# Two-layer recurrent block: final norms and silu at once behind the experts, and 2.3 attention pieces a pair instead of 2

## The chip, the core and the metric

The kernel runs on one core of one Trainium2 chip. TensorE (PE in the profile) multiplies matrices, with its weight loads shown as PEld; VectorE (DVE), ScalarE (ACT) and GpSimd (POOL) work on tiles in the on-chip memory; SyncE (SP) issues most of the transfers. Each engine runs its own instructions in order, and semaphores tie the engines together. The metric is the device time of one execution in microseconds (us).

## What is computed

16 sequences of 256 tokens with 128 values each go through two layers. Each layer normalizes its input, computes a mixer `s` and a mixture of experts `g` from the same normalized input, and adds `s * silu(g)`. The change touches layer 1 alone:

```python
xn = _layernorm(x)
s = _L1_attn_ref(xn, w_qkv, w_proj)          # causal attention, 16 heads of 8, 256 tokens
g = _silu(_L1_ffn_ref(xn, ...))              # 16 experts, two per token
x = x + s * g

def _L1_ffn_ref(x, ...):
    scores = einsum('btd,nd->btn', x, router_w) + router_bias
    topv, topi = top_k(scores, 2)
    weights = softmax(topv)
    ...
    hidden = tanh(mag) * cos(softplus(freq) + 0.1 + bank_phase)
    ...
    out = einsum('tkd,tk->td', sel, weights)
    out = out * rsqrt(mean(out * out, -1) + 1e-6) * norm_w
    return out
```

So the expert half needs a sum over a token's two experts, a norm of that sum and a silu; only then does it meet the attention's `s`, in a product, and `x` in a sum.

## The kernel before

All 4096 tokens are held as 8 blocks of 512 (`NB`), each block as 4 tiles of 128 tokens (`NTL`). `xs[b]` is a block of `x`, `xns[b]` its normalized form (128 of the 130 values of a row of `xnx[b]`), `xnTs[b]` that form transposed. `s_sbs[b]` is another view of the memory of `xnTs[b]`: once a block's attention is done, its `s` takes the place of the transposed input.

Layer 1 has two streams of work that are independent until the end.

*The attention* is a generator of small pieces, `attention()` (L867). It walks over 32 tiles of queries, each in several steps: scores `Sq` to find the maximum (L923, L933, L935), queries with the maximum built in (L985, L987, L991), scores `Sk` again, transposed (L956), their exponential on ACT (L963) with a triangle cut out by POOL for the diagonal (L966), the weighted values `yx` (L1006, copied at L1011), a transpose and the division by the sums (L1018, L1026, L1028). A step's scores for one tile go out with the transposed scores of the tile two before. Per block there are five projections ahead, and a transpose (`turned`, L1038) and the output projection (`projected`, L1046, which copies `s` at L1047 and adds the block to `done`) behind. A piece is yielded with a kind: 0 for a piece that counts, 1 for an exponential, 2 for a mark without work.

*The experts* (L1103) take 79 slots of 128 rows, each of one expert, in ten batches of 8 (the last has 7). A batch gathers its rows, transposes them (L1110), does the frequency products in pairs of tiles (L1121) with abs, exp and ln on ACT (L1125 to L1127) and five DVE operations (L1129 to L1137), loads ACT's other table (L1141), does the magnitude products with a tanh (L1147, L1152), the sines (L1158), loads the first table again (L1159), multiplies (L1164), does the down products (L1173), weighs them (L1177), and scatters the rows to `yd` in DRAM by indirect DMAs on POOL (L389).

`fill(n)` (L1215) puts `n` counting pieces of attention between the steps of the experts. `fill(n, False)`, used in the tanh stage where the table of the exponential isn't loaded, stops at once where the next piece is an exponential. Per batch it is called once at the transposes, with 1 and with `FILL - 1` for every pair in the frequency stage, with `1, False` for every pair in the tanh stage, once behind the sines, and once for each four tiles of the down products. `FILL` is 3. Work that a piece leaves for DVE, such as a maximum, is put into `later` and goes out ahead of the next piece. The order on PE, DVE, ACT and SP is the order in which the Python code issues the instructions; POOL's is held by explicit dependencies.

Behind the experts, `give` sends out the remaining scatters. Then the blocks are finished (`finished`, L1182), in four stages with a `yield` after each: load both results of every token (`results`, L439; the load waits for all scatters of the layer); sum them and take the squares (L1187, L1191) and the factor of the norm (L1192, L1193); scale (L1196), work out the sigmoid in three ACT operations (L1199 to L1201) and multiply by `s` (L1202); multiply by the sigmoid (L1204), add `x` (L1205) and send the block out (L1206). `staged` (L197) runs these as a pipeline: each step of it admits one more block, if `ready` allows, and advances all that are under way by a stage. `ready` asks that the block's attention is done. One step follows every three pieces of attention; what is left when the pieces run out is run behind them.

Of the kernel before, what the change touches and what calls it, by code (L numbers as in the profile page):

```python
# [10 lines left out]
F32 = mybir.dt.float32  # L11
# [3 lines left out]
ALU = mybir.AluOpType  # L15
# [3 lines left out]
P = 128  # L19
D = 128  # L20
# [3 lines left out]
NTL = BT // P  # L24
# [11 lines left out]
SLT = (2 * 4096 + E1 * (P - 1)) // P  # L36
DX = D + 2
WROW = 2 * H1 + 2 * D + 2
FILL = 3
RATE = 0.93  # L40
NEG = -3.0e38
INV2PI = 1.0 / (2.0 * math.pi)
# [10 lines left out]
def ib(ap, n):  # L53
    s = list(ap.shape)
    return ap.unsqueeze(len(s)).to_broadcast(s + [n])
# [3 lines left out]
def two_layer_kernel(  # L59
# [7 lines left out]
    nc = tc.nc  # L67
    NT = x.shape[0]
    NB = NT // BT
# [4 lines left out]
    ov = out.rearrange("(b t p) d -> b p t d", p=P, t=NTL)  # L74
    xs = [cst.tile([P, NTL, D], F32, tag=f"x{b}", name=f"x{b}") for b in range(NB)]

    xnx = [cst.tile([P, NTL, DX], F32, tag=f"xnx{b}", name=f"xnx{b}") for b in range(NB)]
    xns = [t[:, :, 0:D] for t in xnx]
    xnTs = [cst.tile([P, BT], F32, tag=f"xnT{b}", name=f"xnT{b}") for b in range(NB)]

    s_sbs = [t.rearrange("p (t d) -> p t d", t=NTL) for t in xnTs]
# [115 lines left out]
    def staged(gens, ready=lambda b: True):  # L197

        gens, live, b = list(gens), [], 0
        while gens or live:  # L200
            if gens and ready(b):
                live.append(gens.pop(0))
                b += 1
            live = [g for g in live if next(g, g) is not g]
            yield
# [22 lines left out]
    def starts(pool, ne):  # L228

        rm = pool.tile([P, ne * NT32], F32, tag="rt_rm", name="rm")  # L230
        nc.gpsimd.memset(rm, 1.0)
        nc.gpsimd.memset(rm[:, 0 : ne * NT32 : NT32], 0.0)
        return rm
# [197 lines left out]
    def spread():  # L431

        turn[:] = [not turn[0]]
        if wanted and (turn[0] or not given):
            fetch(1)
        else:
            give(1)

    def results(pool, lay, b, tag="gg"):  # L439

        gg = pool.tile([P, 2, NTL, D], F32, tag=tag, name="gg")
        for c in range(2):
            r0 = c * 4096 + b * BT
            got = nc.sync.dma_start(gg[:, c], yds[lay][r0 : r0 + BT, :].rearrange("(t p) d -> p t d", p=P))
            for give in gives[lay]:
                tc.add_manual_dep(got.ins, give.name, SYNC, reason="results in rows")
        return gg
# [31 lines left out]
    with ExitStack() as cg:  # L479
# [307 lines left out]
        with tc.manual_schedule(engines={ET.Activation, ET.PE, ET.DVE, ET.SP}):  # L787
# [15 lines left out]
            hp = hp0.enter_context(tc.tile_pool(name="ghp", bufs=2, side="right"))  # L803
# [21 lines left out]
    with ExitStack() as c1:  # L825
# [261 lines left out]
        def weights_of(j0, n):  # L1087

            wts = []
            for j in range(j0, j0 + n):  # L1090
                reg = tile_expert(emap1, j, E1)
                wt = hp.tile([P, WROW], F32, tag="wt", name="wt", bufs=CPB + 1)
                nc.sync.dma_start(wt, bank[bass.ds(reg, 1)].rearrange("e p w -> p (e w)"))
                wts.append(wt)
            return wts

        def rows_of(j0, n):

            xg = hp.tile([P, n, DX], F32, tag="xg", name="xg")
            wanted.extend((xg, 1, j0 + i, i) for i in range(n))  # L1100
            return xg

        def experts(j0, n, wts, xg, fill):  # L1103
# [12 lines left out]
            for i0 in range(0, n, 2):  # L1116
                m = 2 * min(2, n - i0)
                pf = pf_.tile([P, 4, P], F32, tag="pf", name="pf")
                for k in range(m):
                    i, c = i0 + k // 2, k % 2  # L1120
                    nc.tensor.matmul(  # L1121
                        pf[:, k, :], wts[i][:, c * P : (c + 1) * P], xgTs[i // 4][:, i % 4, :], start=True, stop=True
                    )
                z = hp.tile([P, 4, P], F32, tag="z", name="z", bufs=2)
                nc.scalar.activation(z[:, :m, :], pf[:, :m, :], AF.Abs)  # L1125
                nc.scalar.activation(z[:, :m, :], z[:, :m, :], AF.Exp, scale=-1.0)
                nc.scalar.activation(z[:, :m, :], z[:, :m, :], AF.Ln, bias=1.0)  # L1127
                fill(1)
                nc.vector.scalar_tensor_tensor(z[:, :m, :], pf[:, :m, :], 0.0, z[:, :m, :], ALU.max, ALU.add)  # L1129
                v = hp.tile([P, 4, P], F32, tag="v", name="vt", bufs=CPB // 2 + 1)  # L1130
                for i in range(m // 2):
                    ks = slice(2 * i, 2 * i + 2)
                    nc.vector.scalar_tensor_tensor(  # L1133
                        v[:, ks, :], z[:, ks, :], INV2PI, ib(wts[i0 + i][:, WROW - 2 :], P), ALU.mult, ALU.add
                    )
                nc.vector.tensor_scalar(z[:, :m, :], v[:, :m, :], MAGIC, MAGIC, ALU.add, ALU.subtract)  # L1136
                nc.vector.tensor_tensor(v[:, :m, :], v[:, :m, :], z[:, :m, :], ALU.subtract)  # L1137
                vs.append(v)
                fill(FILL - 1)

            nc.scalar.preload_act_table_set(TRIG)  # L1141
            for i0 in range(0, n, 2):
# [36 lines left out]
                )  # L1179
                given.extend((og, 1, j0 + i, i) for i in range(i0, i0 + n4))  # L1180

        def finished(b):  # L1182

            gg = results(hp, 1, b, "xg")
            yield
            acc = hp.tile([P, NTL, D], F32, tag="v", name="acc1", bufs=CPB // 2 + 1)
            nc.vector.tensor_tensor(acc, gg[:, 0], gg[:, 1], ALU.add)  # L1187
            sq = hp.tile([P, NTL, D], F32, tag="th", name="sq1", bufs=CPB // 2 + 1)
            ss = hp.tile([P, NTL], F32, tag="ss", name="ss1")
            for t in range(NTL):  # L1190
                nc.scalar.activation(sq[:, t, :], acc[:, t, :], AF.Square, accum_out=ss[:, t : t + 1])  # L1191
            nc.scalar.activation(ss, ss, AF.Ln, bias=eps6, scale=1.0 / D)  # L1192
            nc.scalar.activation(ss, ss, AF.Exp, scale=-0.5)  # L1193
            yield
            for t in range(NTL):
                nc.vector.scalar_tensor_tensor(  # L1196
                    acc[:, t, :], acc[:, t, :], ss[:, t : t + 1], sb_nw, ALU.mult, ALU.mult
                )
            nc.scalar.activation(sq, acc, AF.Exp, scale=-1.0)  # L1199
            nc.scalar.activation(sq, sq, AF.Ln, bias=1.0)  # L1200
            nc.scalar.activation(sq, sq, AF.Exp, scale=-1.0)  # L1201
            nc.vector.tensor_tensor(acc, acc, s_sbs[b], ALU.mult)  # L1202
            yield
            nc.vector.tensor_tensor(sq, sq, acc, ALU.mult)  # L1204
            nc.vector.tensor_tensor(sq, xs[b], sq, ALU.add)  # L1205
            nc.sync.dma_start(ov[b], sq)  # L1206
            yield

        wk_ = c1.enter_context(tc.tile_pool(name="l1wk", bufs=2, side="right"))
        pS = c1.enter_context(tc.tile_pool(name="l1pS", bufs=2, space=PSUM))  # L1210
        ps = c1.enter_context(tc.tile_pool(name="l1ps", bufs=2, space=PSUM))
        pf_ = c1.enter_context(tc.tile_pool(name="l1pf", bufs=2, space=PSUM))
        pieces, ahead, later, done = attention(), [], [], set()

        def fill(n, exps=True):  # L1215

            k = 0
            while k < n:
                spread()
                kind, f = ahead.pop() if ahead else next(pieces, (3, None))  # L1220
                if kind != 1:
                    while later:
                        later.pop(0)()
                if kind == 3:
                    return False
                if kind == 1 and not exps:
                    ahead.append((kind, f))
                    return True
                if f is not None:
                    f()  # L1230
                k += kind == 0
            return True

        ET = mybir.EngineType
        with tc.manual_schedule(engines={ET.Activation, ET.PE, ET.DVE, ET.SP}):
            nc.scalar.preload_act_table_set(LN_EXP)

            c_ps[:] = [pf_, "pf"]
            for _ in cstream:
                fill(3)  # L1240
            with tc.tile_pool(name="rt1", bufs=1) as rt1:
                for _ in route(rt1, pf_, sc1, E1, SLT, 1, emap1, starts(rt1, E1), "pf", {"tag": "pf"}):
                    fill(1)
            ccmb.close()
            hp = c1.enter_context(tc.tile_pool(name="l1h", bufs=2))
            batches = [(j0, min(CPB, SLT - j0)) for j0 in range(0, SLT, CPB)]
            got = weights_of(*batches[0]), rows_of(*batches[0])
            fetch(len(wanted))
            for k, (j0, n) in enumerate(batches):
                now, got = got, None  # L1250
                if k + 1 < len(batches):
                    got = rows_of(*batches[k + 1])
                experts(j0, n, *now, fill)
                fetch(len(wanted))
                if got:
                    got = weights_of(*batches[k + 1]), got
            give(len(given))
            ends = staged([finished(b) for b in range(NB)], lambda b: b in done)
            while fill(3):
                next(ends, None)  # L1260
            for _ in ends:
                pass


# [51 lines left out]
```

## Time and profile before

| | us |
|---|---|
| median of 3 runs | 1236.36 |
| lowest and highest run | 1234.08, 1241.92 |
| the profiled execution | 1251.36 |
| its span, first to last instruction | 1249.60 |
| mean granted TensorE clock | 0.843 |

Busy time over the whole span is 910.2 us on PE (73%), 646.3 on PE's weight loads (52%), 769.5 on DVE (62%), 588.7 on ACT (47%) and 390.2 on POOL (31%).

The places in the span that matter here, all in us from its start:

| | us |
|---|---|
| first transposes of the experts (L1110) | 681.0 |
| second L1177 of the first batch, of the last | 736.6, 1135.4 |
| last scatter issued (L389) | 1142.9 |
| first sum of a block's results (L1187) | 1149.2 |
| sums of the next five blocks | 1155.4, 1162.3, 1172.2, 1179.1, 1187.3 |
| sums of the last two blocks | 1221.5, 1239.0 |
| last output projection's copy (L1047) | 1236.2 |
| last output transfer issued (L1206) | 1246.2 |

A busy share is an average over stages that have different limits. So the page of the profile is read first for the whole, and then by windows, where each stage shows which engine has no time left. Where none has, the chain of waits and the timelines show who waits for whom.

### The profile page before, as it was taken

To read this page: it belongs to the slowest core of one execution; us is meant where nothing else is said; L and a number is where in the kernel's file an instruction comes from. 1 tells how busy PE (TensorE), PEld (TensorE's weight loads), DVE (VectorE), ACT (ScalarE), POOL (GpSimd) and SP (SyncE) were. 2 spreads that over 40 slices of the span, in tenths; PEclk is the share of its full clock that TensorE was granted. 3 is DMA by queue.
4 is the path that set the end of the run, shared out by engine and by line. 5 is a ranking of instruction groups with operands and counts; after the bars stand their busy time and mean duration, and the time that the engine had idled before them with its cause. 6 is when DMAs were issued, how large, how long until landed. Compare 5 with 4: busy or idle time off the path is not lost. (4 is left out here: it accounts for less than half of the span.)

```text
span 1249.6 us, 17774 instructions
## 1 busy us (share of the span) xinstructions
PE 910.2 (73%) x6394; PEld 646.3 (52%) x6394; DVE 769.5 (62%) x1442; ACT 588.7 (47%) x1059; POOL 390.2 (31%) x422
## 2 busy tenths in 40 slices
PE   6756478878787773767374887878897889888673
PEld 4334256666566652554142565566565656665342
DVE  5675455646455546736886655756765766675853
ACT  3331267665657462431131455544454655544643
POOL 2000235454455320000103333633652553443120
PEclk9967689899889885677777887988988989899776
DMA  4040248842333202100403030431331333122211
GB/s 112 1 69 1 64 107 211 165 111 72 97 99 106 62 15 88 51 1 1 69 1 129 20 119 18 136 116 33 124 125 48 100 129 117 25 94 66 84 35 34
DMA packets 88415, 95.41 MB, mean 76 GB/s; under 512 B 22228, under 2 KB 64040, under 8 KB 88328
## 3 DMA queue, kind: packets, MB, share of 16 engines
q1 hardware_dynamic: 78632, 74.32, 21.9%
q0 software_dynamic: 9696, 19.97, 6.1%
q8 instruction: 50, 0.82, 0.3%
q14 instruction: 37, 0.30, 0.1%
HBM read 78.03 MB, written 22.51 MB: 80 GB/s over the span
## 5 line engine op out<-in xcount | busy, mean ns | idle before, releaser
L389 POOL DMA_INDIRECT yd<-og,row x150 | 153.8, 1025 | 240.9 <-DVE og L758 116.6
L377 POOL DMA_INDIRECT xg<-xnd,tok x150 | 148.9, 993 | 155.0 <-DVE yT L646 79.7
L956 PE MATMUL Sk<-qm,kT 32*128 32x256 f32 x768 | 129.1, 460 | 43.3 <-ACT pr L963 20.5
L966 POOL TENSOR_SCALAR_AFFINE_SELECT pr<-pr 128x1024 f32<-128x1024 f32 x64 | 72.0, 1125 | 275.7 <-ACT pr L963 275.3
L963 ACT ACTIVATE pr<-Sk 128x1024 f32<-128x1024 f32 x96 | 97.8, 1019 | 96.9 <-PE Sk L956 94.6
L923 PE MATMUL Sq<-km,qT 32*128 32x256 f32 x768 | 132.6, 457 | 12.1 <-DVE mx L933 4.3
L956 PEld LDWEIGHTS Sk<-qm,kT 32*128 32x128 f32 x768 | 76.2, 214 | 61.7 <-ACT pr L963 29.3
L923 PEld LDWEIGHTS Sq<-km,qT 32*128 32x128 f32 x768 | 70.2, 207 | 58.2 <-issue 35.3
L935 DVE TENSOR_REDUCE negm<-Sq 128x8 f32<-128x1024 f32 x64 | 78.0, 1219 | 30.3 <-PE Sk L956 21.7
L721 PEld LDWEIGHTS pf<-xgT,wt 128*128 128x128 f32 x568 | 77.2, 208 | 31.4 <-issue 15.0
L721 PE MATMUL pf<-xgT,wt 128*128 128x128 f32 x568 | 82.9, 294 | 12.0 <-ACT sg L730 6.3
L726 ACT ACTIVATE sg<-pf,nb 128x128 f32<-128x128 f32 x142 | 44.1, 361 | 62.1 <-PE pf L721 61.2
L737 DVE SCALAR_TENSOR_TENSOR gt<-pf,nb,sg 128x128 f32<-128x128 f32 x142 | 42.8, 344 | 47.1 <-ACT sg L730 47.0
L546 PE MATMUL pq<-xnT,sb_wq 128*128 128x512 f32 x64 | 45.4, 850 | 30.0 <-DVE sp L519 28.5
L917 PE MATMUL Sq<-mq,identb 128*128 128x512 bf16 x128 | 42.0, 412 | 16.7 <-DVE negm L935 10.6
L1129 DVE SCALAR_TENSOR_TENSOR z<-pf,z 128x512 f32<-128x512 f32 (+1 forms) x40 | 27.1, 678 | 43.5 <-ACT z L1127 43.5
L1125 ACT ACTIVATE z<-pf 128x512 f32<-128x512 f32 (+1 forms) x40 | 23.7, 593 | 60.9 <-PE pf L1121 60.9
L1173 PE MATMUL pe<-wt,th 128*128 128x128 f32 x316 | 46.7, 309 | 7.0 <-DVE th L1164 7.0
L1173 PEld LDWEIGHTS pe<-wt,th 128*128 128x128 f32 x316 | 43.4, 220 | 14.0 <-issue 10.9
L754 PE MATMUL pe<-sb_wo,gt 128*128 128x128 f32 x284 | 40.1, 300 | 13.0 <-ACT xgT L700 13.0
L754 PEld LDWEIGHTS pe<-sb_wo,gt 128*128 128x128 f32 x284 | 37.2, 210 | 21.5 <-ACT xgT L700 18.1
L351 PE MATMUL pT<-ohj,ohp 128*128 128x142 bf16 (+1 forms) x128 | 14.7, 275 | 45.4 <-DVE ohj L349 45.4
(269 smaller groups left out, 2114.1 us busy)
## 6 DMA issues: line engine op xcount, KB each, us to landing
wt<-bank SPq DMA_DIRECT2D x79, 385.0 KB
wt<-in_w_dram SPq DMA_DIRECT2D x71, 256.0 KB
gg<-yd SPq DMA_DIRECT2D x32, 256.0 KB
xnd<-xnx SPq DMA_DIRECT2D x16, 260.0 KB
xg<-xnd,tok POOLq DMA_INDIRECT x150, 3.4
yd<-og,row POOLq DMA_INDIRECT x150, 2.5
x<-in_x_dram SPq DMA_DIRECT2D x8, 256.0 KB
bank<-in_freq_dram SPq DMA_DIRECT2D x1, 2048.0 KB
```

The costliest lines, as they stand in the source:

```text
L377: return nc.gpsimd.indirect_dma_start(out=xg[:, i, :], out_offset=None, in_=xnds[lay], in_offset=bass.IndirectOffsetOnAxis(ap=toks[lay][:, ...
L389: give = nc.gpsimd.indirect_dma_start(out=yds[lay], out_offset=bass.IndirectOffsetOnAxis(ap=rows[lay][:, j : j + 1], axis=0), in_=og[:, i, ...
L546: nc.tensor.matmul(pq[:, c], w_[:, h * DK : (h + 1) * DK], xnT, start=True, stop=True)
L721: nc.tensor.matmul(pf[:, c, :], wts[i][:, c * P : (c + 1) * P], xgT[:, i, :], start=True, stop=True)
L726: nc.scalar.activation(sg[:, c, :], pf[:, 2 + c, :], AF.Exp, scale=-1.0, bias=nbs[i][:, 2 + c : 3 + c])
L754: nc.tensor.matmul(pe[:, i, :], gts[i][:, c, :], sb_wo0[:, c, :], start=(c == 0), stop=(c == 1))
L923: nc.tensor.matmul(S[:, c, js, :], qT[part][r, tq], km[r, js, tk], start=not diag, stop=True, skip_group_check=True,)
L935: passed(nc.vector.tensor_reduce(ng, S, AX.X, ALU.max, negate=True))
L956: nc.tensor.matmul(S[:, c, js, :], kT[part][r, tk], qm[r, js, :], start=True, stop=True, skip_group_check=True,)
L963: nc.scalar.activation(pr, S, AF.Exp, scale=scale)
L966: pooled(nc.gpsimd.affine_select(pr_, pr_, pattern=[[0, 8], [1, P]], compare_op=ALU.is_ge, fill=0.0, base=0, channel_multiplier=-1,))
L1173: nc.tensor.matmul(pe[:, i - i0, :], ths[i // 2][:, 2 * (i % 2) + c, :], wts[i][:, 2 * H1 + c * D : 2 * H1 + (c + 1) * D], start=(c == 0), ...
```

## The change

Three things change, all in layer 1.

`FILL` is 2.3, and where `fill(FILL - 1)` gave 2 pieces, a running share now gives 2.3 on average: 2 or 3 pieces, the rest carried on to the next pair.

`finished` is split. `weighed(b)` has its load, sum, norm and sigmoid, and ends with a product of the two into `xns[b]`, whose old content isn't needed any more; it adds the block to `ready`. The new `finished(b)` multiplies that by `s`, adds `x` and sends the block out.

The loop at the end runs `weighed` for all blocks without asking for their attention, one step after every two pieces instead of three, and calls `finished(b)` in order for each block whose attention and weighing have both been issued.

```diff
-FILL = 3
+FILL = 2.3
...
                 vs.append(v)
-                fill(FILL - 1)
+                share[0] += FILL
+                fill(int(share[0]))
+                share[0] -= int(share[0])
...
-        def finished(b):
+        def weighed(b):
...
             nc.scalar.activation(sq, acc, AF.Exp, scale=-1.0)
             nc.scalar.activation(sq, sq, AF.Ln, bias=1.0)
             nc.scalar.activation(sq, sq, AF.Exp, scale=-1.0)
-            nc.vector.tensor_tensor(acc, acc, s_sbs[b], ALU.mult)
-            yield
-            nc.vector.tensor_tensor(sq, sq, acc, ALU.mult)
-            nc.vector.tensor_tensor(sq, xs[b], sq, ALU.add)
-            nc.sync.dma_start(ov[b], sq)
-            yield
+            yield
+            nc.vector.tensor_tensor(xns[b], sq, acc, ALU.mult)
+            ready.add(b)
+            yield
+
+        def finished(b):
+            o = hp.tile([P, NTL, D], F32, tag="z", name="o1", bufs=2)
+            nc.vector.tensor_tensor(o, xns[b], s_sbs[b], ALU.mult)
+            nc.vector.tensor_tensor(o, xs[b], o, ALU.add)
+            nc.sync.dma_start(ov[b], o)
...
+        share, ready = [0.0], set()
...
             give(len(given))
-            ends = staged([finished(b) for b in range(NB)], lambda b: b in done)
-            while fill(3):
+            ends, last, b = staged([weighed(b) for b in range(NB)]), False, 0
+            while b < NB:
+                last = last or not fill(2)
                 next(ends, None)
-            for _ in ends:
-                pass
+                while b in done and b in ready:
+                    finished(b)
+                    b += 1
```

## The prediction

> **What bounds the kernel now.** I read four views, in this order: the busy time by stage, the chain of waits at its end, DVE's timeline behind the experts, and PE's and ACT's there.
>
> The windows, in us, with PE, weight loads, DVE, ACT and POOL, each with its count, then the granted clock and the DMA's share:
>
> ```profile
> 690.00:1135.00 445.00, 369.10 (x3040) 266.44 (x3040) 293.30 (x504) 233.26 (x332) 188.31 (x184) 0.91 0.27 84
> 1149.20:1206.80 57.60, 38.91 (x280) 23.04 (x280) 45.86 (x83) 32.98 (x90) 7.77 (x7) 0.71 0.28 79
> 1206.80:1237.00 30.20, 23.00 (x174) 14.43 (x174) 8.66 (x25) 11.99 (x23) 4.37 (x4) 0.78 0.05 14
> ...
> 1135.00:1144.00 9.00, 8.71 (x83) 5.46 (x86) 5.55 (x9) 2.90 (x4) 6.87 (x8) 1.00 0.14 46
> ```
>
> The experts of layer 1 (690 to 1135) hold PE busy for 83% of their time. From 1149 to 1207 DVE is the fullest engine (45.86 of 57.60): six blocks are finished there beside the attention. From 1207 to 1237 it is PE again.
>
> The chain of waits, at its end (start, length, engine, tile, line):
>
> ```profile
> 1229.89 1.06 DVE acc L1196 x4
> 1230.97 0.64 ACT sq L1199
> ...
> 1235.41 3.47 DMA gg<-yd
> 1238.97 0.70 DVE acc L1187
> 1239.70 1.29 ACT sq L1191 x8
> 1241.57 1.15 DVE acc L1196 x4
> 1242.74 0.64 ACT sq L1199
> 1243.41 0.64 ACT sq L1200
> 1244.07 0.64 ACT sq L1201
> 1244.73 0.70 DVE sq L1204
> 1245.45 0.69 DVE sq L1205
> ```
>
> The end is one block's load, norm and silu, with nothing beside it. None of that except the last two DVE steps needs the attention's result.
>
> DVE's, PE's and ACT's timelines (start, length, line, operation; in brackets the idle time before it and who ended it):
>
> ```profile
> 1149.18 0.69 DVE L1187 TENSOR_TENSOR acc<-gg 128x512 f32<-128x512 f32 x1 [7.10 <-DMA gg<-yd]
> 1154.77 0.69 DVE L1202 TENSOR_TENSOR acc<-acc,xnT 128x512 f32<-128x512 f32 x1 [0.69 <-ACT sq L1199]
> ...
> 1150.53 1.12 PE L1018 MATMUL pyt<-ident,yt 128*128 128x128 f32 x4 [4.86 <-DVE qm L991]
> ...
> 1223.91 1.01 ACT L963 ACTIVATE pr<-Sk 128x1024 f32<-128x1024 f32 x1
> 1236.19 0.59 ACT L1047 COPY xnT<-p_s 128x512 f32<-128x512 f32 x1 [2.16 <-PE p_s L1046]
> ...
> 1224.97 1.93 PE L1006 MATMUL yx<-pr,va 128*32 128x256 f32 x16 [3.06 <-ACT pr L963]
> 1232.93 0.48 PE L1038 MATMUL pyT<-ident,y 128*128 128x128 f32 x1 [2.39 <-DVE y L1028]
> ```
>
> The first block's results come 13.3 us after the last expert product on DVE (1135.9), and DVE stands 7.10 us for them. L1202 overwrites `acc` while ACT's L1199 still reads it: 0.69 us, eight times. Twice a block's norm stands in the attention's way: ACT's squares before the 1223.91 exponential, DVE's L1196 and L1202 before the last transpose.
>
> **Where the attention stands.** I counted its pieces from the code's order: 254 that count in `fill`, with exponentials between them that don't. The ten batches issue 17, 16, 17, 16, 17, 18, 16, 18, 16 and 18, which leaves 47 for the time behind them, the first being the second query projection of block 7. The trace agrees: that matmul (L882) starts at 1135.15, the first on PE behind the experts' last.
>
> **The change, part by part.**
>
> 1. *More attention beside experts.* The second fill of each pair of tiles gives 2.3 pieces on average, not 2: 12 more over 40 pairs. But the tanh stage's `fill(1, False)` returns empty at an exponential, and with the shifted order it does so more often. The same count with the change gives 17, 18, 17, 18, 19, 18, 17, 17, 18, 17: 7 more, not 12. Those seven are what PE does now in 1135 to 1144: 8.71 us of work at clock 1.00, some 9.5 at the experts' 0.91. Nothing hides it surely, since PE is busy 83%. Least: a third falls into PE's 76 us of gaps, +6. Most: a piece costs as much as a whole expert stage divided by its 169 pieces, 445/169 = 2.6 us, +18. I take +10, near the row. The Trainium skill ("Trainium Kernel Development and Optimization", Performance Expectations) holds matmul busy time a bad measure of how near the roof PE is, and weight-load busy a good one. By that the stage is 60% full (266.44/445) and the seven cost perhaps 5 us; the sum below would be 5 us better. I stay with the matmul row, since the engine's queue is in order. Beside this, every batch is rearranged: four batches with 16 pieces each took 48.5, 43.9, 37.6 and 43.1 us (from second product to second product). With a spread of 4.5 us a batch, ten may sum to 10 us either way.
>
> 2. *The first wait.* The order is now 2 pieces, load of block 0, 2 pieces, L1187; before, 3 and 3. The wait for the results (POOL's seven scatters at 1.27 us, their landing, the load's 3.3 us) is unchanged and ends 13.3 us behind the last product, in both. But less stands before L1187: PE can run 6 pieces until then where it ran 8. Queued behind DVE's wait are the maxima, and so PE's next scores and ACT's squares. Against the seven fewer pieces, the wait thus gives back two: 34 pieces remain at its end instead of 39. No time by itself; its price lies in the next part.
>
> 3. *Eight blocks instead of six, beside 16 pieces instead of 21.* From 1149.18 to the end of the last query score (1206.8) DVE worked 45.86 us. Six blocks' finishing in it is some 27 us (L1187 0.69, L1196 1.13 to 1.96, L1202 0.69, L1204 and L1205 1.4 and more), the pieces that now lie ahead of the wait some 4.4, so 14.5 stay for attention. With the change: eight times L1187, L1196 and the new product (2.5) and six times the two final operations (1.4), with 2 us for slow ones as in the trace: 30. Sum 44.5. DVE's idle time was 11.7: 4.2 from L1202's wait, which goes as the product no longer overwrites what ACT reads, and 7 from waiting for PE. I leave 3.5: 48 us, that is -9.5. What is late next is ACT: per block 2.0 us of exponentials, 1.8 of squares and 1.2 of attention, 5 us, against DVE's 5.6 per round. The loads now alternate with output transfers on SP: each load is issued a round (5.6 us) ahead of its use and lands in 3.5, so nothing; without that cover 3.5 us a block. POOL's selects (1.1 us) stand behind the scatters as before. The product's write into rows of 130 values has no row; 0 to 0.1 us each, taken as 0. Bounds of this part: -13 (no idle time) to -4. The lower end is where a rule speaks against the change. After gaps of 4.86 and 3.06 us the trace shows matmuls at 0.80 for 0.48 and at 1.93 for 1.07; clock 0.71 over the stage. The Trainium skill ("TensorE: Matmul & The Clock Gate", Part 1: The HAM clock gate) says that one idle window of about 3.4 us drops the array to half clock and as long a busy one restores it. Rounds with two pieces leave PE idle about half of the time, so by the rule PE stays slow, each round's scores come 0.7 us later, and this part gives -4, the sum -6. I keep the row: the stage has much of that slow clock already, and PE isn't its bound.
>
> 4. *Attention's last 18 pieces.* Block 6's squares no longer delay the exponential of 1223.91 (its scores ended at 1221.9): -2.0. L1196 and L1202 no longer delay the last divide (possible at 1230.1, was 1232.24): -2.1. Block 6's final two operations fit DVE's idle time around 1218. Sum -4.1; perhaps 1.5 more if PE's shorter gap keeps its clock.
>
> 5. *The end.* From the last copy of `s` (1236.78) to the end of the span (1249.6) are 12.8 us. Left are two DVE operations (1.4), semaphores (0.1) and the output transfer, which took 1246.2 to 1249.6, 3.4: 4.9. So -7.9. The loads, squares and exponentials taken from here lie in part 3, counted there.
>
> Sum: +10 - 9.5 - 4.1 - 7.9 = -11.5, with the clock's 1.5 about -13. The profiled execution took 1251.36 (span 1249.60), 15 above the median of the runs shown, 1236.36: profile 1238, median 1223.
>
> **The rivals.**
>
> *The experts stall (slower).* Only one query score and one key score fit PSUM at a time. A third piece between two pairs more often brings a second score, which waits for a maximum on DVE behind L1129 to L1137, itself behind ACT's chain. The trace has such a wait: PE 3.74 us idle before the scores of 1017.10, then slow matmuls (0.80). Were 8 of the 12 third pieces to meet it at 3.7 us: +30 beside the +10, against -21.5 to -23: +18, 1254. It is slower by 1% from 7 such waits on. For it: L956 waits longest for `pr` and `negm`. Against: 40 pairs with three pieces each show few of these gaps now.
>
> *Only the end is gained.* The eight blocks cost in rounds of two pieces what they cost before, part 3 giving nothing: +10 - 4.1 - 7.9 = -2, 1234. For it: DVE and ACT hand each block back and forth three times, and the first wait comes earlier.
>
> *The move is free.* The pieces fill PE's gaps, and batches fall well: +0 for part 1, -23: 1213.
>
> **How the numbers follow.** My forecast has 0.45, the only-end rival 0.25, the free move 0.15, the stall 0.15. The forecast's own uncertainty, mainly the rearranged batches, is some 10 us. The range, 1206 to 1243, takes in the free move and the only-end rival and leaves most of the stall out; the forecast's own is 1213 to 1234. Within 1% (1224 to 1248.7) is about what a measurement can't tell from no change. Faster by more: half of the forecast and its better side, the free move, little of the rest, 0.50. Within: 0.36. Slower: 0.14.
>
> **What would show it.** Right: 7 pieces fewer behind the experts; those about 10 us longer; no L1187 or L1196 behind the last copy of `s`, which is 5 us before the end; DVE over 90% busy from its first wait to the last query score. Wrong: experts longer by over 25 us with L956 waiting for `negm` or `mx`; DVE idle in the rounds for `ss` or `sq`; a load landing late for L1187.

## The result and the profile after

| | us |
|---|---|
| before, median of 20 runs (the 3 shown above among them) | 1241.00 |
| changed kernel, median of 20 runs | 1249.47 |
| ratio, with its 95% interval | 1.0066, 1.0044 to 1.0088 |
| profiled execution of the changed kernel, its span | 1251.8 |

The kernel became slower by two thirds of a per cent, where 1% faster was forecast. (The forecast of 1223 us started from the median of three runs, 1236.36; that of twenty is 1241.00.) The shorter end is there, to about a microsecond. The experts took it back, and more.

Splitting each profiled execution at the second L1177 of the first batch and at that of the last batch gives the two halves of the account. (Between L1137 and L1201 a line of before has a number higher by two in the changed kernel: L1177 is L1179 there.)

| | experts, from first to last batch | behind them, to the end | sum |
|---|---|---|---|
| before | 398.7 | 114.3 | 513.0 |
| changed | 427.4 | 90.4 | 517.8 |
| difference | +28.7 | -23.9 | +4.8 |

The profiled execution of before, 1251.36 us, was 10 us above its median. Most of what it has too much lies ahead of the split: its experts start at 681.0 us, those of the twelve other profiles at 668.5 to 678.3, behind the same code.

The windows of the changed kernel answer to those shown of before (start and end, then busy time and count of PE, weight loads, DVE, ACT and POOL, granted clock, DMA share, GB/s). The first is its expert stage, the second reaches from the first block's sum to the last query score's maximum, the third from there to the last copy of `s`:

```profile
687.40:1161.40 474.00, 385.45 (x3116) 278.02 (x3119) 304.15 (x511) 236.85 (x337) 191.88 (x187) 0.89 0.25 79
1173.90:1223.10 49.20, 35.11 (x226) 19.02 (x226) 45.66 (x88) 36.40 (x113) 6.45 (x5) 0.64 0.36 104
1223.10:1247.00 23.90, 20.91 (x174) 13.63 (x174) 6.87 (x20) 8.97 (x11) 4.50 (x4) 0.88 0.04 12
```

The second window has shrunk from 57.6 to 49.2 us and DVE is 93% busy in it. The third has shrunk from 30.2 to 23.9 with the same 174 matmuls, at a granted clock of 0.88 instead of 0.78. Of the chain of waits, the end is now

```profile
1245.16 1.17 PE p_s L1046 x8
1246.97 0.70 DVE o L1211
1247.70 0.69 DVE o L1212
```

Two DVE operations and the output transfer follow the last output projection and its copy on ACT; no load, norm or sigmoid does.

What the experts lost is seen in who holds up PE. Its longest waits, before (736.6 to 1135.4), and two shorter ones that matter below; the numbers are us in total, times, and the longest:

```profile
PE Sk L956 <- ACT pr L963: 15.1, 10, 3.6
PE Sk L956 <- DVE negm L935: 13.9, 7, 3.1
PE pe L1173 <- DVE th L1164: 7.0, 3, 5.9
PE Sk L956 <- DVE mx L933: 6.8, 4, 3.7
PE pq L882 <- DVE y L1028: 4.7, 3, 2.2
PE pk L888 <- DVE yt L1011: 2.8, 2, 1.6
...
PE pyt L1018 <- DVE qm L991: 1.7, 3, 0.6
PE p_s L1046 <- DVE yt L1011: 1.7, 1, 1.7
```

and after (734.0 to 1161.4):

```profile
PE Sk L956 <- ACT pr L963: 17.2, 11, 3.6
PE pyt L1018 <- DVE qm L991: 9.8, 4, 3.5
PE Sk L956 <- DVE mx L933: 9.7, 6, 2.7
PE Sk L956 <- DVE negm L935: 8.7, 6, 2.3
PE pe L1175 <- DVE th L1166: 7.6, 4, 5.9
PE p_s L1046 <- DVE yt L1011: 7.2, 3, 2.8
PE pk L888 <- DVE yt L1011: 5.1, 2, 3.0
```

The waits for a maximum (`mx`, `negm`) haven't grown in sum. Grown are those of a transpose (L1018) and of projections (L1046, L888) for `qm` and `yt`, from 6.2 to 22.1 us: `qm` and `yt` are what DVE makes when it empties a buffer of PSUM, the memory that PE writes its products into. By the code none of these matmuls reads what it waits for (`pyt` is made from an older `yt`, `p_s` from `yT`, `pk` from the normalized input), and the scores `Sk` don't read `mx` or `negm` either. So each waits for the buffer. One such wait in full. PE's timeline of the changed kernel:

```profile
1028.19 1.06 PE L1121 MATMUL pf<-xgT,wt 128*128 128x128 f32 x8
1029.09 0.60 PE L985 MATMUL pqm<-ident,negm 128*128 128x256 f32 x2
...
1030.06 1.07 PE L1006 MATMUL yx<-pr,va 128*32 128x256 f32 x16
1030.95 1.05 PE L1006 MATMUL yx<-pr,vb 128*32 128x256 f32 x16
1035.47 1.11 PE L1018 MATMUL pyt<-ident,yt 128*128 128x128 f32 x4 [3.47 <-DVE qm L991]
1036.37 1.91 PE L1121 MATMUL pf<-xgT,wt 128*128 128x128 f32 x8
```

and DVE's beside it:

```profile
1031.24 0.69 DVE L1129 SCALAR_TENSOR_TENSOR z<-pf,z 128x512 f32<-128x512 f32 x1 [2.21 <-ACT z L1127]
1031.97 1.65 DVE L1133 SCALAR_TENSOR_TENSOR vt<-z,wt 128x256 f32<-128x256 f32 x2
1033.65 0.43 DVE L1136 TENSOR_SCALAR z<-vt 128x512 f32<-128x512 f32 x1
1034.12 0.69 DVE L1137 TENSOR_TENSOR vt<-vt,z 128x512 f32<-128x512 f32 x1
1034.73 0.68 DVE L991 TENSOR_TENSOR qm<-pqm,qmask 128x512 f32<-128x512 f32 x1
```

`pqm`, `yx` and `pyt` come from one pool of two PSUM buffers. The queries (`pqm`) were the piece of the pair's first fill. Their copy `qm` is deferred work (`later`) and is issued only with the next piece, behind L1129 to L1137. DVE stands 2.21 us at L1129 for ACT, works off the pair's five operations, and only then frees the buffer. PE, which has filled both, waits 3.47 us, and the pair's next products (L1121) follow at 1.91 us instead of 1.06.

The scores meet the same in the kernel before, with two score buffers in place of the general pool's two. Two pieces of one pair hold scores; DVE's timeline has the first's maximum behind the chain, and PE's the wait:

```profile
1011.72 0.69 DVE L1129 SCALAR_TENSOR_TENSOR z<-pf,z 128x512 f32<-128x512 f32 x1 [2.95 <-ACT z L1127]
1015.82 1.22 DVE L933 TENSOR_REDUCE mx<-Sq 128x8 f32<-128x1024 f32 x1
1017.10 0.80 PE L956 MATMUL Sk<-qm,kT 32*128 32x256 f32 x2 [3.74 <-DVE mx L933]
```

This gives theory A: the loss lies in pairs whose pieces need a PSUM buffer back that DVE frees only behind the pair's chain. From the order of the pieces such pairs can be counted. Either the first fill holds queries, weighted values or a divide and the second fill has two more users of that pool, or both fills hold a score. Before: 7 of 40 pairs, all of the second kind. Changed: 18, 8 of the first kind and 10 of the second. Its rivals: B, each further piece costs 3.5 us wherever it stands; C, any new arrangement moves the experts by some 10 us without a rule; and later D, DVE gains in all pairs alike when it has something to do while it waits for ACT.

### The profile page after: what moved, and what is told of

It reads as the page before. It is cut to its first block, busy times and chain, and to the rows that moved or that the text cites. A ratio compares the mean times of both kernels' runs of the same rounds, so it can differ in the third digit from the quotient of the medians.

```text
span 1251.8 us, 17762 instructions
## 1 busy us (share of the span) xinstructions
PE 915.2 (73%) x6394; PEld 650.8 (52%) x6394; DVE 774.8 (62%) x1442; ACT 587.8 (47%) x1059; POOL 393.0 (31%) x422
## 3 DMA queue, kind: packets, MB, share of 16 engines
q1 hardware_dynamic: 78632, 74.32, 21.5%
## 5 line engine op out<-in xcount | busy, mean ns | idle before, releaser
L956 PE MATMUL Sk<-qm,kT 32*128 32x256 f32 x768 | 131.8, 469 | 42.9 <-ACT pr L963 23.6
L923 PE MATMUL Sq<-km,qT 32*128 32x256 f32 x768 | 135.6, 465 | 9.4 <-DVE mx L933 8.4
L935 DVE TENSOR_REDUCE negm<-Sq 128x8 f32<-128x1024 f32 x64 | 78.0, 1219 | 33.2 <-PE Sk L956 22.1
L721 PEld LDWEIGHTS pf<-xgT,wt 128*128 128x128 f32 x568 | 77.2, 207 | 31.4 <-issue 15.8
L721 PE MATMUL pf<-xgT,wt 128*128 128x128 f32 x568 | 82.8, 294 | 12.0 <-ACT sg L730 6.3
L1129 DVE SCALAR_TENSOR_TENSOR z<-pf,z 128x512 f32<-128x512 f32 (+1 forms) x40 | 27.2, 681 | 55.4 <-ACT z L1127 55.4
L1121 PEld LDWEIGHTS pf<-xgT,wt 128*128 128x128 f32 x316 | 46.5, 224 | 9.6 <-issue 8.6
L1121 PE MATMUL pf<-xgT,wt 128*128 128x128 f32 x316 | 51.5, 315 | 0.0
```

What stands on the lines that cost most here:

```text
L721: nc.tensor.matmul(pf[:, c, :], wts[i][:, c * P : (c + 1) * P], xgT[:, i, :], start=True, stop=True)
L923: nc.tensor.matmul(S[:, c, js, :], qT[part][r, tq], km[r, js, tk], start=not diag, stop=True, skip_group_check=True,)
L935: passed(nc.vector.tensor_reduce(ng, S, AX.X, ALU.max, negate=True))
L956: nc.tensor.matmul(S[:, c, js, :], kT[part][r, tk], qm[r, js, :], start=True, stop=True, skip_group_check=True,)
L1121: nc.tensor.matmul(pf[:, k, :], wts[i][:, c * P : (c + 1) * P], xgTs[i // 4][:, i % 4, :], start=True, stop=True)
```

## Experiments: the parts of the change

**The new end alone.** The experts issue two pieces per pair, as before.

```diff
-                share[0] += FILL
-                fill(int(share[0]))
-                share[0] -= int(share[0])
+                fill(2)
```

> The new end with two pieces per pair, as before the change. The experts then issue the same pieces in the same order as before (47 pieces left behind them). If the end's gain is what the two traces show (tail 91.5 us with 40 pieces against 113.7 with 47), seven more pieces at 1.3 to 1.6 us each give a tail of some 102 us: -12 us against before, ratio 0.990. Rival, that the shorter tail is only the seven pieces that moved out of it: -2 us or less, ratio 0.998.

Measured: 1227.30 against 1242.01 us, ratio 0.9867 (0.9845 to 0.989). The experts took 396.5 us, as before (398.7), and the rest 97.9 instead of 114.3. So the end is worth 16 us by itself with all 47 pieces still behind the experts, and taking seven pieces out of it brings only 7.5 more (97.9 to 90.4): 1.1 us a piece.

**The share alone.** The kernel before with 2.3 instead of 2 pieces.

```diff
-FILL = 3
+FILL = 2.3
...
-                fill(FILL - 1)
+                share[0] += FILL
+                fill(int(share[0]))
+                share[0] -= int(share[0])
```

> 2.3 pieces per pair with the old end. If the experts' +24 us come with the pieces, they are there again, and seven pieces fewer in the old tail give back some 10: +14 us, ratio 1.011. If they came from somewhere else in the change: -1 us, ratio 0.999.

Measured: 1257.09 against 1242.01 us, ratio 1.0112 (1.0087 to 1.0136). Experts 426.7 us, the rest 97.0. The loss in the experts comes with the share, and the old end gains 17 from the seven pieces fewer, more than the 10 expected. The two gains at the end don't add: 16 us by the new end alone, 17 by the seven pieces alone, 24 by both.

**The same pieces at another place.** New end, two pieces per pair, and the further piece at each batch's transposes.

```diff
                 if i0 == 0:
-                    fill(1)
+                    fill(2)
```

> The new end, two pieces per pair, and two pieces instead of one at each batch's transposes. By the count of pieces each batch issues exactly as many as in the changed kernel (18, 18, 17, 18, 19, 18, 17, 17, 18, 17) and 40 are left. Theory A, the place decides (a third piece in a pair's second fill needs a PSUM buffer that DVE only frees behind the pair's chain): the experts cost about +10 us instead of +24, ratio to before 0.990. Theory B, each further piece costs 3.5 us wherever it stands: as the changed kernel, 1.006. Theory C, any new arrangement moves the experts by some 10 us without a rule: anything from 0.985 to 1.01, and only the trace's gaps can say which.

Measured: 1232.24 against 1242.01 us, ratio 0.9917 (0.9898 to 0.9937). Experts 406.9 us, the rest 90.4. Each batch issues as many pieces as in the changed kernel, and the experts are 20.5 us shorter. That is against B. Against the new end alone the seven pieces cost 10.4 us beside the experts and save 7.5 behind them: even in the better place the move gains nothing. By the count 12 pairs are short of a buffer here, five more than with the new end alone, and the 40 pairs together, measured from the first L1121 product of one to that of the next (behind a batch's fourth pair, to the first L1147), are only 5.1 us longer. So a short pair seems to have no fixed price; what the pieces would cost here without stalls wasn't run.

## Experiments: the deferred work

**Deferred work first.** The changed kernel, with DVE's copies and maxima that the pair's first fill left issued ahead of L1129.

```diff
                 fill(1)
+                while later:
+                    later.pop(0)()
                 nc.vector.scalar_tensor_tensor(z[:, :m, :], pf[:, :m, :], 0.0, z[:, :m, :], ALU.max, ALU.add)
```

> The changed kernel, and the DVE work left by the pair's first piece is issued ahead of L1129 instead of behind L1137, so the PSUM buffer comes free before the pair's chain. Theory A: the gaps of PE before transposes and projections that waited for qm and yt (some 20 us in the experts) go, experts 10 to 15 us shorter than in the changed kernel, ratio to before 0.995 to 0.998. Theory B and C: no more than 5 us either way, or worse, because DVE then waits for PE ahead of L1129 and L1129 to L1137 come later.

Measured: 1203.13 against 1242.01 us, ratio 0.9667 (0.9639 to 0.9694). Experts 384.4 us, the rest 90.2 as in the changed kernel. The expected size was far too small: 43 us, not 10 to 15. The same three pieces at the same place, in PE's timeline of this kernel, where the two lines make L1131 of L1129:

```profile
989.23 0.60 PE L985 MATMUL pqm<-ident,negm 128*128 128x256 f32 x2
...
991.09 1.05 PE L1006 MATMUL yx<-pr,vb 128*32 128x256 f32 x16
992.07 0.66 PE L1018 MATMUL pyt<-ident,yt 128*128 128x128 f32 x4
992.56 1.06 PE L1121 MATMUL pf<-xgT,wt 128*128 128x128 f32 x8
```

and DVE's:

```profile
990.31 0.69 DVE L991 TENSOR_TENSOR qm<-pqm,qmask 128x512 f32<-128x512 f32 x1 [1.14 <-PE pqm L987]
991.39 0.69 DVE L1131 SCALAR_TENSOR_TENSOR z<-pf,z 128x512 f32<-128x512 f32 x1 [0.38 <-ACT z L1127]
```

The copy now stands in the time in which DVE waited for ACT anyway. From `pqm` to the next products are 3.3 us, where there were 7.3, and those products run at 1.06.

But this alone doesn't separate A from D, as DVE gets work into its waits in every pair. Further runs do.

**The same on the kernel before**, with the same two lines added and nothing else.

> The kernel before with nothing but DVE's deferred work issued ahead of L1129. By the count of pieces 7 of its 40 pairs hold a piece whose PSUM buffer another piece of the same pair needs back before DVE reaches the deferred work (18 in the changed kernel, 12 with the extra piece at the transposes). Theory A, those pairs make the loss: the changed kernel won 45 us over 18 pairs, 2.5 each, so here -17 us, ratio 0.986. Theory D, DVE merely fills its waits for ACT in all pairs alike, whatever the pieces: as much as with the change, -43 us, 0.965.

Measured: 1219.89 against 1242.42 us, ratio 0.9824 (0.9791 to 0.9857). Experts 375.2 us instead of 398.7, the rest 114.2; the profile is that of the fastest of six runs. That is between A and D, nearer to A. The PE timelines of the two kernels show where the 23.5 us come from. Measured in the same way, the 7 pairs are 19.5 us shorter together, and the other 33 are 1.0 longer. So the kernel before had lost time there too, but half as much.

**Only in the 18 pairs, and only in the other 22**, of the changed kernel; `STALL` is the list of (batch, pair) from the count. Against the kernel with the deferred work first in all pairs (in the second run, `not in`):

```diff
-                while later:
+                while later and (j0 // CPB, i0 // 2) in STALL:
```

> The changed kernel with the deferred work ahead of L1129 only in the 18 pairs counted as short of a buffer. Theory A: most of the 45 us, ratio 0.972 to 0.976. Theory D: 18 of 40 pairs, 20 us, ratio 0.990.

> The changed kernel with the deferred work ahead of L1129 only in the other 22 pairs. Theory A: at most 10 us, ratio 0.999 to 1.006. Theory D: 22 of 40 pairs, 25 us, ratio 0.986.

Measured: in the 18 pairs, 1205.73 against 1242.42 us, ratio 0.9698 (0.966 to 0.9736), experts 384.8 us. In the other 22, 1254.15 against 1242.42, ratio 1.0082 (1.005 to 1.0114), experts 436.8 in the profile, which is that of the slowest of six runs. The 18 pairs bring the whole gain within the intervals, and the other 22 none. That is A against D, and against C: pairs that were picked from the order of the pieces carry the loss. No run gave the pools a third buffer, which would be another way to ask.

PE's waits with the deferred work first in the 18 pairs (in both kernels the lines ahead of L1129 have numbers higher by one than in the changed kernel, those behind it by three):

```profile
PE Sk L957 <- ACT pr L964: 14.9, 9, 3.6
PE pe L1178 <- DVE th L1169: 7.6, 4, 5.9
PE Sq L924 <- DVE negm L936: 6.7, 4, 2.8
```

and with it in the other 22:

```profile
PE Sk L957 <- DVE mx L934: 13.1, 7, 4.5
PE pyt L1019 <- DVE qm L992: 9.8, 3, 3.5
PE Sk L957 <- DVE negm L936: 8.5, 5, 2.5
...
PE p_s L1047 <- DVE yt L1012: 5.6, 2, 2.8
```

The waits for `qm` and `yt` stay in the second and are not among the longest of the first.

**The two kinds of pairs apart.** `PAIRS` holds the 8 pairs of the general pool, or the 10 of the scores.

```diff
+                while later and (j0 // CPB, i0 // 2) in PAIRS:
+                    later.pop(0)()
```

> The changed kernel with the deferred work ahead of L1129 only in the 8 pairs where queries, weighted values or a divide hold one of the two buffers of the general PSUM pool and two more pieces want one. If the pairs are alike (2.5 us each): -20 us against the changed kernel, ratio 0.990. If this kind is the dearer one, since its gaps before L1018, L1046 and L888 are up to 3.5 us long and followed by a slow clock: -30, ratio 0.982.

> The same only in the 10 pairs where a second score of the pair needs the PSUM tile of the first, whose maximum is deferred (the rival of the prediction on record). If the pairs are alike: -25 us, ratio 0.986. If the other kind is the dearer one: -15, ratio 0.994.

Measured: the 8 pairs 0.9886 (0.9845 to 0.9928), experts 406.2 us; the 10 pairs 0.985 (0.9817 to 0.9883), experts 402.8 us. Against the changed kernel's 427.4 that is 21.2 and 24.6 us, 2.7 and 2.5 a pair, and the two sum to 45.8, about what all 18 together bring (42.6). The two kinds are alike on average, and their effects add. That the waits for maxima hadn't grown in sum against before thus didn't mean that they were cheap: they were a cost in both kernels.

**The parts put together.** New end, two pieces per pair, deferred work first.

> The new end, two pieces per pair, DVE's deferred work ahead of L1129: the best of the parts. Theory A: 7 such pairs, so 17 us below the new end alone, ratio 0.973. Theory D: 43 below it, 0.952. If pieces without a stall cost the same beside experts and behind them (1.1 to 1.2 us each), it equals the changed kernel with deferred work first, 0.967.

Measured: 1207.63 against 1242.42 us, ratio 0.9719 (0.9689 to 0.9748). Experts 375.2, the rest 99.7, a sum of 474.9 against 474.6 for the changed kernel with the deferred work first. Against the new end alone the 7 pairs are again shorter together, by 19.6 us, and the other 33 are 1.2 longer. Freed of these stalls, the seven pieces cost 9.2 us beside the experts and save 9.6 behind them.

> The changed kernel with the deferred work issued first at three places: ahead of L1129, ahead of the products L1164 (DVE waits for the sines there) and ahead of L1177 (DVE waits for PE). If deferred work behind a wait of DVE costs PE's buffers there as well, some 5 to 10 us below the kernel with the first place alone: ratio 0.960. If only the place ahead of L1129 holds up PE: 0.967.

The further edits are the same two lines behind the `fill(1)` of the sines and of the down products. Measured: 1204.92 against 1244.03 us, ratio 0.9681 (0.9645 to 0.9717): nothing beyond the first place. The changed kernel with the deferred work first (0.9667) is the fastest measured, and this one and the one without the share can hardly be told from it.

## Why the prediction was wrong

*The step that failed is part 1, "I take +10, near the row".* The experts became 28.7 us longer, beyond the bound of +18 as well. The count of seven more pieces was right (the first batch issues 18, not 17, but in both kernels), and so was their own price, 9.2 us with the deferred work first. Missing were the stalls, with 18 pairs instead of 7 short of a buffer: putting the deferred work first takes 43.0 us out of the changed kernel's experts and 23.5 out of those of before. The difference is 19.5, and 9.2 + 19.5 = 28.7. I took a piece's time on PE for its price, and treated what a new order does to the waits as a spread of either sign. It wasn't: the order decides which pieces meet in a pair, and so how many pairs wait for what DVE has deferred. The third piece itself is the smaller part of this. By the count only 7 of the 18 pairs would have buffers enough without it; the other 11 are short because the pieces now fall into other pairs.

*The stall rival had the place, the sign and half of the mechanism.* It forecast +18 and stood at 0.15. Second scores waiting for a deferred maximum behind L1129 to L1137 are what the 10 pairs show. The other 8 were not in it: the general PSUM pool and its copies. Its size was too large: +40 in the experts against 28.7, and +18 in all against 8.5 by the medians. That its 1254 us lies near the 1249.47 measured is in part luck, as it started from a base 4.6 us too low. The argument against it, that three pieces per pair showed few such gaps, misread the trace. The waits for `negm` and `mx` were there, and the deferred work first was worth 23.5 us in the experts of the kernel before, most of it in its 7 pairs. The same order of pieces that gave the seven could have given these pairs too.

*The other value weighed in part 1*, from the weight loads' busy time, would have missed by more: the 40% of the time without weight loads did not take up the pieces.

*Part 2 holds nearly.* The first block's sum starts 12.4 us behind the start of the last L1179; before, it was 13.8 us behind the last L1177, and I had taken that as unchanged. DVE stands 7.27 us for it.

*Part 3 holds:* 49.2 us, forecast 48, was 57.6. The clock in this window did fall, to 0.64 from 0.71. But the part came to -8.4, near the -9.5 forecast and not the -4 that I had worked out for a slow PE: DVE, not PE, fills this window.

*Part 4 holds with its optional term:* from the end of the last query score's maximum to the end of the last copy of `s` went from 30.0 to 23.9 us, -6.1 against -4.1 and perhaps 1.5 more. The exponential no longer waits for squares, and the weighted values behind it take 1.07 us for the half that took 1.93.

*Part 5 holds:* 4.9 us from the last copy of `s` to the end, forecast 4.9.

Parts 3 to 5 sum to -21.5, or -23 with the clock. The time behind the experts fell by 23.9.

*That only the end is gained, and that the move is free,* are both refuted by the same split.

## What to carry to other kernels

When independent work is interleaved by counting pieces, check the place of each piece's PSUM release, not only its engine time. If the release is deferred, or stands in the order of its engine behind an operation that waits for a third engine, then one piece more between two of the host's steps can use up the pool and stop the busiest engine; another order of the same pieces can do it too. Issue the copies that free buffers ahead of such a wait; here two lines did more than all the rest of the change. And try a shorter end and a moved share of work separately: the end alone gave -1.3%, the move alone +1.1%.

## What was not expected of the hardware

A stall of PE costs more than its own gap. In the experts of the changed kernel PE's idle time is some 12 us above that of before (427.4 - 349.2 against 398.8 - 332.3), and its busy time 17 us above:

```profile
734.00:1161.40 427.40, 349.17 (x2833) 252.66 (x2835) 274.92 (x459) 213.43 (x305) 181.06 (x177) 0.89 0.27 84
```

With the deferred work first, the same 2833 matmuls are busy for

```profile
727.20:1111.50 384.30, 328.60 (x2833) 238.50 (x2835) 274.84 (x459) 212.80 (x305) 181.27 (x177) 0.92 0.29 93
```

so of the 43 us between the two, 21 are the same matmuls busy for longer, and 22 are gaps. DVE's busy time is the same to 0.1 us. The clock may account for most of the 21. By the profile's clock records, PE had half its clock for 92 us of the changed kernel's experts, in 19 stretches, and for 61 us, in 13, with the deferred work first. The slow products shown above took 1.91 us for 1.06, nearly twice as long, so 31 us more of such work cost up to 15. In both kernels each of these stretches begins within 7 us of a gap of over 1 us. What makes up the rest of the 21 is open.
